# Who shifts the last rows: VectorE in place of ScalarE and GpSimd, and an earlier table load, in a two-layer kernel on one core

## The chip, the core and the metric

The kernel runs on one core of one Trainium2 chip. A core has a matrix engine (TensorE, PE in the profile), three engines for elementwise work (VectorE or DVE, ScalarE or ACT, GpSimd or POOL), SyncE (SP), which here only issues transfers, and 16 DMA engines that move data between the memory of the chip and the core. Each engine works through its own queue in order, and the engines wait for one another through semaphores. The metric is the device time of one execution in microseconds; lower is better.

## What is computed

Four sequences of 512 rows and 512 columns, all in 32-bit floats, go through two layers. The first is attention followed by two wide blocks with GELU; the second is an adapter whose weights are chosen per sequence by an index, with a residual and a normalisation over each row. Cut to what matters:

```python
def layer0(x, codes, Wq, Wk, Wv, Wp, bp, cW1, cb1, cW2, cb2, mW1, mb1, mW2, mb2):
    attn = softmax((x @ Wq) @ (x @ Wk).T * 512 ** -0.5)
    attn_out = attn @ (x @ Wv) @ Wp + bp
    cms_out = gelu(attn_out @ cW1 + cb1) @ cW2 + cb2 + one_hot(codes, 512)[:, None, :]
    modifier = gelu(concat([attn_out, cms_out]) @ mW1 + mb1) @ mW2 + mb2
    return clip(x + cms_out + modifier, 0.0, 1.0)

def layer1(stream, x, W_down, b_down, W_up, b_up, ln_w, ln_b):
    Wd, bd, Wu, bu, g, b = (p[stream] for p in (W_down, b_down, W_up, b_up, ln_w, ln_b))
    h = x + gelu(x @ Wd + bd) @ Wu + bu
    mean, var = h.mean(-1), h.var(-1)
    return (h - mean) * rsqrt(var + 1e-5) * g + b
```

The change lies in the last line of `layer1`: each row is shifted by its mean, scaled by `g` and by the reciprocal root of its variance, and `b` is added ("the shift").

## The kernel before, in words

The kernel works on the four sequences in two pairs. It computes the products of the first layer by nested seven-product schemes, so that sums and differences of blocks (on VectorE and GpSimd) take the place of part of the matrix work. For each pair the wide blocks follow one another, and behind them each of the pair's two sequences goes through the adapter. The adapters of the first pair are spread between the matrix work of the second pair. Those of the second pair stand at the end of the program: one is begun inside the last wide block (`adapter`, lines 1534 to 1545, sequence 3), and the other, sequence 2, comes after everything else (`last_adapter`, lines 1547 to 1557). That last one is the sequence of the change.

An adapter first applies the down projection and a GELU (`down`, line 1483: four matmuls per tile on TensorE, then the GELU on ScalarE at line 1493). In the last sequence the tokens are halved, so there are four GELUs of 128 x 256. Then come four row tiles of 128 rows each. For each tile, `up` (line 1495) has TensorE add the turned residual and the up projection in a bank of PSUM, and VectorE take the statistics (lines 1514 and 1516) and write (h - mean) * g to SBUF in one instruction (line 1517). Next `normalised` (line 1520) has ScalarE take the root of the variance (line 1523) and VectorE its reciprocal (line 1526). What follows depends on the tile:

- tiles 0, 1 and 2: ScalarE multiplies the 128 x 512 tile by the reciprocal root (line 1530), then GpSimd adds `b` (line 1531);
- tile 3 (`t == NT - 1`): VectorE does both in one instruction (line 1528).

Last, the tile of 256 KB is sent to the output (line 1532). In the second pair the issuing engine is SyncE, and its eight issues stand in its queue in the order of the tiles.

ScalarE needs a table of values for GELU and another for roots, and a load (ACT_TABLE_LOAD) stands in its queue where the function changes. In the last sequence the load for the roots is recorded with the first root at line 1523, behind the wait for that tile's statistics. A scheduler orders the queues of the engines; `tc.keep_in_program_order` keeps an instruction at the place where it was written. `touched` is a column of 128 values that is written once at the start and never read. The end of the program has line 1713: every engine drains its queue, SyncE waits for the outputs, and a barrier over all engines closes the program.

Of the kernel before, what the change touches and what calls it, by code (L numbers as in the profile page):

```python
# [10 lines left out]
AF = mybir.ActivationFunctionType  # L11
# [7 lines left out]
def kernel(  # L19
# [38 lines left out]
    nc = tc.nc  # L58
# [5 lines left out]
    NT = T // P  # L64
# [16 lines left out]
    def bank(name):  # L81
        return psum.tile([P, 512], F32, tag="bank", name=name)
# [100 lines left out]
    eps = const.tile([P, 1], F32, name="eps")  # L183
    nc.vector.memset(eps, EPS)

    touched = const.tile([P, 1], F32, name="touched")
# [1291 lines left out]
    def with_bias(y, bu, y1):  # L1478

        for c in range(NV):  # L1480
            nc.scalar.activation(y1[:, c, :], y[:, c, :], AF.Identity, bias=bu[:, c : c + 1])

    def down(y, wd, bd, g, n, tokens=slice(0, 512)):
        ps = bank("down_ps")[:, : tokens.stop - tokens.start]
        for c in range(NV):
            nc.tensor.matmul(  # L1486
                ps,
                lhsT=wd[:, c, n * P : (n + 1) * P],
                rhs=y[:, c, tokens],
                start=(c == 0),  # L1490
                stop=(c == NV - 1),
            )
        nc.scalar.activation(g[:, n, tokens], ps, AF.Gelu, bias=bd[:, n : n + 1])

    def up(g, wu, y1, aff, h, t):


        ps = bank("up_ps")
        for c in range(NV):
            nc.tensor.matmul(  # L1500
                ps[:, c * P : (c + 1) * P], lhsT=y1[:, c, t * P : (t + 1) * P], rhs=ident,
                is_transpose=True, start=(c == 0), stop=True, skip_group_check=True,
            )
        for n in range(NB):
            nc.tensor.matmul(  # L1505
                ps,
                lhsT=g[:, n, t * P : (t + 1) * P],
                rhs=wu[:, n, :],
                start=False,
                stop=(n == NB - 1),  # L1510
                skip_group_check=True,
            )
        stats = small.tile([P, 6], F32, name="stats")
        nc.vector.bn_stats(stats, ps)
        mv = small.tile([P, 2], F32, name="mv")
        nc.vector.bn_aggr(mv, stats)
        nc.vector.scalar_tensor_tensor(h, ps, mv[:, 0:1], aff[:, 0, :], ALU.subtract, ALU.mult)
        return mv

    def normalised(b, h, mv, aff, t, eng, last=False):  # L1520

        rstd = small.tile([P, 1], F32, name="rstd")
        root = nc.scalar.activation(rstd, mv[:, 1:2], AF.Sqrt, bias=eps)
        if last:
            tc.keep_in_program_order(root)
        nc.vector.reciprocal(rstd, rstd)
        if t == NT - 1:
            nc.vector.scalar_tensor_tensor(h, h, rstd, aff[:, 1, :], ALU.mult, ALU.add)
        else:
            nc.scalar.activation(h, h, AF.Copy, scale=rstd)  # L1530
            nc.gpsimd.tensor_tensor(h, h, aff[:, 1, :], ALU.add)
        eng.dma_start(out=out[b, t * P : (t + 1) * P, :], in_=h)

    def adapter(b, y, loaded, g, rows, y1, eng):

        wd, wu, bd, bu, aff = loaded
        for n in range(NB):
            down(y, wd, bd, g, n)
            yield
        with_bias(y, bu, y1)  # L1540
        yield
        for t in range(NT):
            mv = up(g, wu, y1, aff, rows[:, t, :], t)
            normalised(b, rows[:, t, :], mv, aff, t, eng)
            yield

    def last_adapter(b, y, loaded, g, rows, y1, eng):

        wd, wu, bd, bu, aff = loaded
        with_bias(y, bu, y1)  # L1550
        first_half, second_half = slice(0, 256), slice(256, 512)
        for tokens in (first_half, second_half):
            for n in range(NB):
                down(y, wd, bd, g, n, tokens)
        for t in range(NT):
            mv = up(g, wu, y1, aff, rows[:, t, :], t)
            normalised(b, rows[:, t, :], mv, aff, t, eng, last=True)
# [14 lines left out]
    for pair in range(B // 2):  # L1572
# [87 lines left out]
        if final:  # L1660
            for _ in one:
                pass
            adapt(0, spaces[0], nc.sync, kind=last_adapter)
        else:
            load(0, 6)
            c1_rhs = next_rhs[0]
            extra = adapters()
# [49 lines left out]
```

## Time and profile before

| what | us |
|---|---|
| three runs | 1176.99, 1177.01, 1180.69 |
| median of the runs | 1177.01 |
| the profiled execution, its own time | 1178.76 |
| span of the profiled execution (first to last instruction) | 1176.8 |
| busy in the span: TensorE matmuls | 1163.0 (99%) |
| busy: VectorE | 880.6 (75%) |
| busy: GpSimd | 578.2 (49%) |
| busy: ScalarE | 297.4 (25%) |

The granted TensorE clock was 0.998 of full speed. A line of the profile's timeline gives the start in the span, the busy time, the engine, the line of the program, the operation, the tile written and the tiles read, and the count; in brackets stands the idle time before it and what ended it. A line of the chain gives a start, a time, and what that time was spent on. A row for one source line gives the engine (with a q for the engine's instruction queue alone), the operation, the count, the shortest, median and longest duration in ns, and the first and last start in us.

### The profile page before, as it was taken

What the parts mean: (1) busy time and instruction counts of PE and PEld (TensorE: products, weight loads), DVE (VectorE), ACT (ScalarE), POOL (GpSimd) and SP (SyncE); (2) the same over time, 40 slices, a digit from 0 to 9 for tenths busy, and PEclk for the clock granted to TensorE, in tenths of its full rate; (3) what the DMA queues carried; (4) which work ended last, traced back from release to release, by engine and by line L of the source; (5) the groups of instructions that cost most, each with busy time, mean ns of one, the idle gap of its engine ahead of it and who ended that gap; (6) DMA issues with size and microseconds to landing.
All of it is one profiled execution on the core that took longest, in us unless ns stands there. A gap on an engine that the chain in (4) does not pass through costs nothing.

```text
span 1176.8 us, 13556 instructions
## 1 busy us (share of the span) xinstructions
PE 1163.0 (99%) x4937; PEld 918.0 (78%) x4937; DVE 880.6 (75%) x1192; ACT 297.4 (25%) x540; POOL 578.2 (49%) x634
## 2 busy tenths in 40 slices
PE   9999999999999999999999999999999999999996
PEld 8588558657468888888888877748888888888874
DVE  5745655587699867899699956769994588689954
ACT  4235315236520000013310036380000003220024
POOL 4989999988986057997400723630000001143002
PEclk9999999999999999999999999999999999999999
DMA  9642784897766588999937654262745364684701
GB/s 337 254 147 107 285 338 162 298 398 269 265 251 244 185 271 313 339 366 330 294 127 303 198 179 170 83 195 107 287 146 193 145 243 151 187 296 173 239 1 71
DMA packets 82609, 263.07 MB, mean 224 GB/s; under 512 B 8132, under 2 KB 37872, under 8 KB 67312
## 3 DMA queue, kind: packets, MB, share of 16 engines
q1 hardware_dynamic: 57184, 155.21, 36.8%
q0 software_dynamic: 23120, 97.57, 23.5%
q10 hardware_dynamic: 2240, 9.44, 2.0%
q8 instruction: 39, 0.64, 0.2%
q14 instruction: 26, 0.21, 0.1%
HBM read 190.88 MB, written 68.16 MB: 220 GB/s over the span
## 4 chain that ended last, share of the span: by engine, by line
PE 95%; DVE 2%; DMA 1%; ACT 1%; issue 0%
PE i L1380 29%; PE i L1282 26%; PE sum L704 9%; PE sum L638 8%; PE c L1214 8%; PE sum L1139 7%; PE up_ps L1505 2%; PE down_ps L1486 2%; PE tr_ps L490 1%; DMA wslot<-in_L_cond_mW 1%; PE up_ps L1500 1%; DVE hidden L548 1%; DVE slot L210 1%; PE tr_ps L869 0%; PE idle_ps L193 0%
## 5 line engine op out<-in xcount | busy, mean ns | idle before, releaser
L1282 PE MATMUL i<-slot,wslot 128*128 128x256 f32 x1184 | 261.8, 379 | 1.8 <-DVE part L1009 1.4
L1282 PEld LDWEIGHTS i<-slot,wslot 128*128 128x128 f32 x1184 | 224.6, 190 | 33.7 <-issue 2.4
L1380 PE MATMUL i<-slot,wslot 128*128 128x256 f32 x896 | 202.5, 379 | 0.0
L1380 PEld LDWEIGHTS i<-slot,wslot 128*128 128x128 f32 x896 | 170.2, 190 | 23.1
L1016 ACT COPY first<-i 128x256 f32<-128x256 f32 (+1 forms) x56 | 26.8, 478 | 523.7 <-PE i L1380 250.8
L1380 PE MATMUL i<-hidden,wslot 128*128 128x256 f32 x576 | 132.2, 379 | 0.0
L1380 PEld LDWEIGHTS i<-hidden,wslot 128*128 128x128 f32 x576 | 109.4, 190 | 16.2 <-issue 1.4
L1009 DVE TENSOR_TENSOR part<-i,part 128x512 f32<-128x512 f32 (+1 forms) x156 | 90.8, 592 | 39.1 <-PE i L1282 24.6
L1038 ACT ACTIVATE hidden<-hidden,bias 128x512 f32<-128x512 f32 x128 | 84.4, 716 | 76.4 <-DVE hidden L548 66.8
L1603 POOL DMA_DIRECT2D slot<-xT_kept x4 | 2.9, 715 | 165.2 <-PE i L1282 165.2
L1214 PE MATMUL c<-slot,wslot 128*128 128x512 f32 x160 | 69.2, 592 | 0.0
L210 DVE TENSOR_TENSOR slot<-hidden 128x1024 f32<-128x1024 f32 x48 | 62.2, 1296 | 0.0
L1606 POOL TENSOR_TENSOR cms<-cms,slot 128x512 f32<-128x512 f32 x16 | 26.0, 1643 | 70.9 <-PE i L1282 38.5
L1214 PEld LDWEIGHTS c<-slot,wslot 128*128 128x128 f32 x160 | 30.4, 190 | 38.3 <-issue 35.6
L210 DVE TENSOR_TENSOR slot<-hidden,slot 128x1024 f32<-128x1024 f32 x48 | 59.3, 1235 | 0.3
L1009 DVE TENSOR_TENSOR part<-i,first 128x512 f32<-128x512 f32 (+1 forms) x62 | 36.4, 591 | 28.6 <-PE i L1282 17.4
L548 DVE TENSOR_TENSOR sum<-sum,wslot 128x512 f32<-128x512 f32 x48 | 33.4, 697 | 31.0 <-PE sum L704 18.9
L548 DVE TENSOR_TENSOR hidden<-part,hidden 128x2048 f32<-128x2048 f32 x20 | 55.5, 2776 | 0.5
L704 PE MATMUL sum<-hidden,wslot 128*128 128x256 f32 x232 | 53.2, 379 | 0.0
L1139 PE MATMUL sum<-mod,wslot 128*128 128x256 f32 x224 | 51.8, 379 | 0.0
L704 PEld LDWEIGHTS sum<-hidden,wslot 128*128 128x128 f32 x232 | 43.8, 190 | 5.8
L1139 PEld LDWEIGHTS sum<-mod,wslot 128*128 128x128 f32 x224 | 42.6, 190 | 5.8
(329 smaller groups left out, 2099.8 us busy)
## 6 DMA issues: line engine op xcount, KB each, us to landing
wslot<-m_kept SPq DMA_DIRECT2D x48, 1024.0 KB
wslot<-m_kept SPq DMA_DIRECT2D x36, 512.0 KB
wslot<-c_kept SPq DMA_DIRECT2D x16, 1024.0 KB
slot<-in_L_cond_mW POOLq DMA_DIRECT2D x24, 512.0 KB
wslot<-in_L_cond_mW SPq DMA_DIRECT2D x24, 512.0 KB
wslot<-in_L_cond_cW SPq DMA_DIRECT2D x36, 256.0 KB
slot<-in_L_cond_cW POOLq DMA_DIRECT2D x16, 512.0 KB
m_kept<-wide POOLq DMA_DIRECT2D x6, 1024.0 KB
```

The source lines that it names most:

```text
L210: i = eng.tensor_tensor(out_, one, two, ALU.subtract)
L548: nc.vector.tensor_tensor(dst, a, b, ALU.add)
L638: nc.tensor.matmul(ps, lhsT=lhs[p][:, c, r * P : (r + 1) * P], rhs=rhs[p][:, c, :], start=(first_ and c == 0), stop=(c == 1), skip_group_c ...
L704: nc.tensor.matmul(v[:, j, :], lhsT=lhs[p][:, c, j * P : (j + 1) * P], rhs=rhs[p][:, c, :], start=(first_ and j == 0 and c == 0), stop=(c ...
L1009: nc.vector.tensor_tensor(dst, ps, other, ALU.add)
L1016: nc.scalar.copy(c1, p1)
L1038: nc.scalar.activation(block[:, t, :], block[:, t, :], AF.Gelu, bias=bias_c[:, 8 * half + t : 8 * half + t + 1],)
L1139: nc.tensor.matmul(halves_of(ps)[:, j, :], lhsT=a[g][:, at_[q], j * P : (j + 1) * P], rhs=rhs[q][:, 0, :], start=(first_ and j == 0), stop ...
L1214: nc.tensor.matmul(ps, lhsT=lhs(c, t), rhs=operands[p][:, c, :], start=(c == 0), stop=(c == 1),)
L1282: nc.tensor.matmul(out_ps[:, j, :], lhsT=a[j][q][:, c, :], rhs=now[q][:, c, :], start=(c == 0), stop=(c == 1),)
L1380: nc.tensor.matmul(ps[:, :256], lhsT=a[k // 2][q][:, k % 2, :], rhs=now[q][:, k, :], start=(k == 0), stop=(k == 3),)
L1606: nc.gpsimd.tensor_tensor(cms[s][:, d, :], cms[s][:, d, :], in_rows[3][:, d, :], ALU.add)
```

## The change

In the last sequence, VectorE's single instruction is used for tiles 1, 2 and 3 and no longer for tile 3 alone; tile 0 stays with ScalarE and GpSimd. And a root of the constant `eps` into `touched` is written behind the last GELU of the last sequence, kept at that place, so that the table for the roots is loaded there. The other three sequences are as before.

```diff
@@ normalised @@
         if last:
             tc.keep_in_program_order(root)
         nc.vector.reciprocal(rstd, rstd)
-        if t == NT - 1:
+        if t == NT - 1 or last and t > 0:
+
             nc.vector.scalar_tensor_tensor(h, h, rstd, aff[:, 1, :], ALU.mult, ALU.add)
         else:
             nc.scalar.activation(h, h, AF.Copy, scale=rstd)
@@ last_adapter @@
         for tokens in (first_half, second_half):
             for n in range(NB):
                 down(y, wd, bd, g, n, tokens)
+
+        tc.keep_in_program_order(nc.scalar.activation(touched, eps, AF.Sqrt))
         for t in range(NT):
             mv = up(g, wu, y1, aff, rows[:, t, :], t)
             normalised(b, rows[:, t, :], mv, aff, t, eng, last=True)
```

In the built program the order on TensorE and SyncE is unchanged. ScalarE has the table load and the added root directly behind the fourth GELU, and two multiplies fewer. VectorE has two more instructions, each behind its tile's reciprocal, and the reciprocal of tile 0 now stands ahead of the statistics of tile 1 and no longer behind them. GpSimd has two adds fewer.

## The prediction

> **What bounds the kernel now.** I read four views, from the whole to the end: the page, the chain of work that ended last, the instructions in order of time from 1158 us on, and the rows of line 1713, the closing of the program, in short windows. Where a view rounds a row to 0.1, I read its start from the trace to 0.01. The change touches nothing ahead of the last sequence's four row tiles, so only the last 18 us can move.
>
> The page puts the kernel on TensorE, and the chain says how that hands over at the end:
>
> ```profile
> span 1176.8 us, 13556 instructions
> ...
> PE 95%; DVE 2%; DMA 1%; ACT 1%; issue 0%
> ```
> ```profile
> 1165.67 1.73 PE up_ps L1505 x4
> 1167.41 0.02 issue
> 1167.43 0.71 DVE stats L1514
> 1168.14 0.02 issue
> 1168.17 0.19 DVE mv L1516
> 1168.36 0.03 issue
> 1168.38 0.36 DVE hidden L1517
> 1168.75 0.30 issue
> 1169.05 0.16 DVE rstd L1526
> 1169.21 0.03 issue
> 1169.24 0.75 DVE hidden L1528
> ```
>
> TensorE stops at 1167.41, and VectorE finishes tile 3 at 1169.24 + 0.75 = 1169.99. The span is 1176.8, so 6.8 us lie behind the last arithmetic, and the chain is silent on them. Line 1713 fills them:
>
> ```profile
> L1713 SPq EVENT_SEMAPHORE  x10: 17/28/28, 1170.4 to 1172.4; - x10
> L1713 SPq DRAIN  x2: 7/7/7, 1172.5 to 1172.5; - x2
> L1713 PEldq DRAIN  x1: 5360/5360/5360, 1162.1 to 1162.1; - x1
> L1713 POOLq DRAIN  x1: 8172/8172/8172, 1167.8 to 1167.8; - x1
> L1713 ACTq DRAIN  x1: 326/326/326, 1168.4 to 1168.4; - x1
> L1713 DVEq DRAIN  x1: 791/791/791, 1169.3 to 1169.3; - x1
> ```
>
> Here is the number that decides. Every engine drains before the closing barrier. SyncE, which waits for the last output to land, is through at 1172.5. ScalarE is through at 1168.7, VectorE at 1170.0, TensorE at 1167.5. GpSimd's drain takes 8.17 us and ends at 1167.85 + 8.17 = 1176.02; the barrier's first rows on GpSimd stand at 1176.1, the span's end at 1176.8. So **GpSimd's drain ends last, 3.5 us after SyncE**. The view of waits puts 3.7 us of SyncE's wait there down to TensorE's queue, which had been idle since 1167.5: the name is wrong, the wait is real.
>
> The drain is that of GpSimd's own queue. Its row starts when the last add (line 1531, tile 2) goes to the engine; that add runs from 1167.88 for 1.26 us, to 1169.14. The drain therefore lasts 6.87 us beyond the last add. The drain with which the program opens (line 1702) took 167 ns, so the long one is not a price of every drain; why this one is long, no row shows.
>
> **The change, part by part.** All durations are from the last tiles in order of time.
>
> *Table load.* Before, it stands behind the wait for tile 0's variance: 1161.96 to 1163.24. After, ScalarE issues it behind its last GELU (1158.81 + 0.47 = 1159.28): 1.28 us, then one 128x1 root of a constant, 0.29 (as the root at line 1523), done by about 1160.9. Tile 0's variance comes at 1161.88, so both are covered by 2.7 us of idle time that ScalarE has there; nothing but the roots is queued behind them. Tile 0's root runs at about 1161.97 to 1162.27 instead of 1163.25 to 1163.55.
>
> *Tile 0.* VectorE's shift-and-scale (line 1517) starts at 1161.92 as before; the reciprocal follows 0.67 later, as on tile 2 (1166.23 to 1166.90), ending at 1162.74. ScalarE's multiply then takes 0.72 (1162.77 to 1163.49) and GpSimd's add 1.26: **1163.57 to 1164.83**. It is now GpSimd's last work. Before, GpSimd ended at 1169.14; it ends 4.3 us earlier. In the program's order VectorE's reciprocal of tile 0 now stands ahead of tile 1's statistics, so it could hold them; it ends 0.4 before they can start (1163.12, set by TensorE).
>
> *Tiles 1 and 2.* Removed: two ScalarE multiplies (0.72 each) and two GpSimd adds (1.26 each). Added: two VectorE instructions of the form at line 1528, 0.75 each. Tile by tile VectorE now needs what tile 3 took, 1167.43 to 1169.99 = 2.56, against TensorE's 2.16 per tile (1163.12, 1165.28). So VectorE falls behind. Tile 1: 1163.12 to 1165.68. Tile 2's statistics do not depend on the row ahead of them; they start between 0.08 before it ends (as the reciprocal at 1169.05 does before 1169.13) and 0.04 after: 1165.60 to 1165.72, and the tile ends at 1168.16 to 1168.28. Tile 3 likewise starts at 1168.08 to 1168.32 and ends at **1170.64 to 1170.88**, 0.65 to 0.89 later than before. I take 0.7, since the pipelined start is what a pair with no dependence shows. The roots stay hidden beside the shift-and-scale (0.3 beside 0.67).
>
> *Outputs.* All eight output issues of the last pair are on SyncE, in order; tiles 1 and 2 now wait for VectorE instead of GpSimd. Issues: 1164.9, 1165.7, 1168.2, 1170.7. Each of these transfers moves data for about 0.85 us, starting 0.85 after its issue (windows from 1166.5 on), so the last one was not queued before and is not after. No other queue is touched: GpSimd issues no DMA here, and its indirect loads ended at 1092.
>
> *The end.* SyncE: from the last row of VectorE to its drain 1172.55 - 1169.99 = 2.56, so 1170.7 + 2.56 = 1173.26. GpSimd: 1164.83 + 6.87 = 1171.70, now 1.6 us early. SyncE ends last. From the later of the two to the span's end it was 1176.8 - 1176.02 = 0.78; the span becomes 1174.0, **2.8 us less**.
>
> So the change loses 0.7 us on the chain that the profile names and gains 3.5 on the one it does not. The profiled execution took 1178.76 for its span of 1176.8 (1.96 around it), 1.75 above the median of the three runs, 1177.01. 1178.76 - 2.8 = 1175.96 for an execution like that one; from the median, **1174.3** (2.76 less, rounded up).
>
> Unknown is the drain's rule. From the nearest rows its excess lies between 0.05 (the opening one, which ended at 0.49, behind a last memset that ended at 0.44) and 6.87; only an excess above 1173.26 - 1164.83 = 8.4 would make it bind again. I take 6.87, from the same place in the same program.
>
> The Trainium skill (VectorE: DVE Perf Modes, The DRAIN you can't avoid) speaks against this: it calls the drains at a program's start and end boilerplate of about 12 ns on all five engines. By that rule GpSimd's drain would cost nothing, SyncE would have closed the program before as well, and the sum would be +0.7 instead of -2.8. The trace has 7 ns for SyncE's and 8172 ns for GpSimd's, so for GpSimd the forecast follows the row; what is left of the rule is in the first rival.
>
> **Rivals.**
> - *The drain follows something common, not GpSimd's last add* (slower): it ended 3.5 after SyncE's and 6.0 after VectorE's last row, and one execution cannot tell these distances apart. If it keeps one of them, the whole end moves with VectorE's tile 3 by 0.7: 1177.7. It decides whenever the drain ends more than 1.6 us later than 1171.7. For it: nothing shows what the drain does for 6.87 us. Against: the profile shows no wait of it for another engine, and nothing else runs between 1172.6 and 1176.0 that could release it. Chance 0.13. (A drain that costs nothing by itself and only shows the wait for such a common thing, as the rule above would have it, is this case too.)
> - *The drain is tied to the last add, but not by a steady 6.87*: shorter in the timed runs than in the profiled one (which took 1.75 more than their median), so that less was there to gain, or longer now. Half the gain: 1175.8. Chance 0.12.
> - *The change does not do what it says*: the built order shows the load directly behind the fourth GELU and the three rows on VectorE. Were the load still late, GpSimd's add would end 1.1 later and its drain at 1172.8, still ahead of SyncE's 1173.3, so the time would be the same 1174.3. Chance 0.02, counted with the forecast.
> - *Something outside the change*: one of the three runs shown is 1180.69, 3.7 above the others; a median drawn there gives about 1178. Chance 0.05.
>
> **How the numbers follow.** The forecast, 1174.3, has 0.70, with its own range 1173.6 to 1175.0 (0.65 to 0.89 on VectorE, some tenths for the landing and the barrier). To leave no more than 2 in 10 out the range must reach the first rival: 1173.5 to 1177.8. 0.3% is 3.5 us, about what a measurement of this kernel can tell from no change, and the most that this change can gain is those 3.5 us if VectorE lost nothing. So faster by over 0.3% has 0.10 (the forecast, if the drain was longer in the runs than in the profile), slower 0.04 (most of the last rival), within it the remaining 0.86.
>
> **What would show it.** GpSimd's last add near 1163.6, its drain ending near 1171.7; VectorE's last row ending at 1170.6 to 1170.9; SyncE's drain near 1173.3, now the last; a span of 1174.0. If GpSimd's drain still ends after SyncE's, the step "6.87 behind the last add" is wrong. If VectorE ends later than 1170.9, something holds it that I don't see: GpSimd's tile 0 add, which ends 0.1 before tile 1's new row starts, is the candidate.

## The result, and the profile after

| | before | after |
|---|---|---|
| median of 22 runs each, us | 1177.0 | 1176.03 |
| lowest and highest run | 1176.15 to 1180.69 | 1173.07 to 1178.75 |
| profiled execution | 1178.76 | 1176.32 |
| its span | 1176.8 | 1174.2 |

The ratio of the runs is 0.998, with a 95% interval of 0.9972 to 0.9989: a gain of 0.1 to 0.3%, within the 0.3% that the prediction could not tell from no change. The two medians alone would give 0.9992, which lies outside that interval; the section on the other two microseconds says why. The forecast was 1174.3 in a range of 1173.5 to 1177.8. The median lies in the range, 1.7 above the forecast.

The page of the kernel after gives the span:

```profile
span 1174.2 us, 13555 instructions
```

The chain of waits of the kernel after, its last pieces (start, time, what it was spent on):

```profile
1167.66 0.75 DVE hidden L1529
1168.42 0.62 DVE stats L1514
...
1170.03 0.08 DVE rstd L1526
1170.11 0.02 issue
1170.13 0.75 DVE hidden L1529
```

Before, the chain went from TensorE's four matmuls into the statistics of tile 3. Now a row of VectorE (tile 2's, line 1529) stands ahead of those statistics: VectorE is the engine that is late in the last tiles, as the working said. VectorE ends at 1170.13 + 0.75 = 1170.88, where it had ended at 1169.99.

The closing of the program, now line 1716, in a window from 1160 to 1173.6 us:

```profile
L1716 SPq DRAIN  x2: 7/7/7, 1173.4 to 1173.4; - x2
L1716 POOLq EVENT_SEMAPHORE  x2: 17/17/17, 1173.4 to 1173.5; - x2
L1716 POOLq DRAIN  x1: 8182/8182/8182, 1163.8 to 1163.8; - x1
```

GpSimd's drain is as long as before (8182 ns, 8172 before) but starts 4.0 us earlier, at 1163.805. It ends at 1171.99, and SyncE's drain, at 1173.42, is now the last. The barrier's rows on GpSimd follow at once; before, SyncE was through at 1172.5 and the barrier had to wait until 1176.0 for GpSimd.

The timeline of the kernel after, the rows that the change moved:

```profile
1159.57 1.28 ACT L1557 ACT_TABLE_LOAD   x1
1160.87 0.20 ACT L1557 ACTIVATE touched<-eps 128x1 f32<-128x1 f32 x1
...
1163.84 1.27 POOL L1532 TENSOR_TENSOR hidden<-hidden,wide 128x512 f32<-128x512 f32 x1 [9.94 <-ACT hidden L1531]
...
1165.20 0.75 DVE L1529 SCALAR_TENSOR_TENSOR hidden<-hidden,rstd,wide 128x512 f32<-128x512 f32 x1
```

The load stands in idle time ahead of tile 0's statistics (1161.24 here). GpSimd's one add ends at 1165.12, and the first of VectorE's new rows starts 0.08 behind that end. This neighbourhood will matter.

**A ruler for the rest.** The statistics of tile 0 in the last sequence (line 1514) are the first instruction that any of these changes can delay. I call what lies ahead of that row *the head* and what lies from its start to the span's end *the tail*:

| profiled execution | head | tail | GpSimd's drain ends | SyncE's drain |
|---|---|---|---|---|
| before | 1160.97 | 15.84 | 1176.02 | 1172.55 |
| after | 1161.24 | 12.96 | 1171.99 | 1173.42 |

The tail became 2.88 shorter. The raw spans differ by 2.6 because the head came out 0.27 longer, and it holds the same instructions in both kernels, but for the early load and its root, which run while ScalarE has nothing else to do.

### The profile page after: what moved, and what is told of

Same layout as the page of the kernel before. It is cut to its first block, busy times and chain, and to the rows that moved or that the text cites. A ratio compares the mean times of both kernels' runs of the same rounds, so it can differ in the third digit from the quotient of the medians.

```text
span 1174.2 us, 13555 instructions
## 1 busy us (share of the span) xinstructions
PE 1163.1 (99%) x4937; PEld 918.1 (78%) x4937; DVE 876.7 (75%) x1194; ACT 296.3 (25%) x539; POOL 574.2 (49%) x632
## 4 chain that ended last, share of the span: by engine, by line
PE 94%; DVE 2%; DMA 2%; ACT 1%; issue 0%
PE i L1380 29%; PE i L1282 25%; PE sum L704 9%; PE sum L638 8%; PE c L1214 8%; PE sum L1139 7%; PE down_ps L1486 2%; DMA wslot<-in_L_cond_mW 2%; PE up_ps L1505 2%; PE tr_ps L490 1%; DVE hidden L548 1%; DVE slot L210 1%; PE up_ps L1500 1%; PE tr_ps L869 0%; PE idle_ps L193 0%
```

## The experiments

My theory: GpSimd's drain closes the program, 6.87 behind GpSimd's last add, so what helps is that GpSimd stops early; the table load is worth nothing by itself. The rivals: the early load carries part of the gain; and the drain follows something other than GpSimd's own last work. A second set of questions is what the 6.87 us are. Twelve kernels ran. All times of the large kernels' ends are given as tails.

### The two halves of the change

The early load alone, from the kernel after:

```diff
-        if t == NT - 1 or last and t > 0:
+        if t == NT - 1:
```

> The table load behind the last GELU is kept; the tiles 0, 1 and 2 are shifted by ScalarE and GpSimd as before. Theory (GpSimd's closing drain ends 6.9 us behind its last add, and that drain ended last before): GpSimd's last add is again that of tile 2, ending near 1169.1, since tile 2 waits for TensorE and not for the table; its drain ends near 1176.0; the time is that of the kernel before, within 0.3 us. Rival (the earlier table is what shortened the kernel): about 2.6 us below the kernel before, as the changed kernel.

The tail is 15.84, that of before to 0.01. The drain of GpSimd (its closing is line 1715) binds as before:

```profile
L1715 SPq DRAIN  x2: 7/7/7, 1173.8 to 1173.9; - x2
L1715 POOLq DRAIN  x1: 8175/8175/8175, 1169.2 to 1169.2; - x1
```

SyncE is through at 1173.9, GpSimd at 1177.39. The median of 12 runs is 1177.12 against 1178.59 for before on that chip (31 runs); the ratio, 0.9991, has an interval of 0.9978 to 1.0003, which includes 1 but reaches down to the rival's 2.6 us. So it is the tail, and not the runs, that settles it: the load alone gains nothing there.

The rows alone, with the table load where it was, behind the wait for tile 0's variance:

```diff
-        tc.keep_in_program_order(nc.scalar.activation(touched, eps, AF.Sqrt))
```

> VectorE shifts the tiles 1, 2 and 3; the table load is back behind the wait for tile 0. Theory: GpSimd's last add (tile 0) ends 1.1 us later than in the changed kernel, near 1166.0, its drain near 1172.9, still ahead of SyncE's 1173.4; the time is that of the changed kernel, within 0.3 us, 2.6 below the kernel before. Rival (the earlier table is what shortened the kernel): the time of the kernel before, or 0.7 above it.

The tail is 13.81, 2.03 better than before but 0.85 worse than after. My expectation missed this. (The runs, with a median of 1176.68 and a ratio of 0.9985, 0.9973 to 0.9996, do not tell it from the change.) The timelines of GpSimd and of VectorE in this kernel show why:

```profile
1164.89 1.26 POOL L1532 TENSOR_TENSOR hidden<-hidden,wide 128x512 f32<-128x512 f32 x1 [11.09 <-ACT hidden L1531]
```
```profile
1165.23 1.47 DVE L1529 SCALAR_TENSOR_TENSOR hidden<-hidden,rstd,wide 128x512 f32<-128x512 f32 x1
1166.63 0.69 DVE L1514 BATCH_NORM_STATS2 stats<-up_ps 128x6 f32<-128x512 f32 x1
```

With the late load, GpSimd's add of tile 0 comes some 1.1 later relative to VectorE and lies beside tile 1's row. The row takes 1.47 instead of 0.75. It also starts 0.13 later than in the kernel after, since with the late load ScalarE's root of tile 1 comes later; so the statistics of tile 2 behind it start 0.86 late, 0.72 of it from the stretch. VectorE, which has no slack in these tiles, carries that to the end: SyncE's drain stands at 1174.19, the drain of GpSimd at 1173.03. In the kernel after, the same row starts 0.08 behind the end of the add and takes 0.75. So the load does have a worth, but mainly not the one that its place suggests: it takes GpSimd's add out of VectorE's way.

The Trainium skill (SBUF — State Buffer, SBUF: two separate sides) states a rule for such pairs: VectorE and GpSimd share one pair of ports to SBUF, as a lock that is held for a whole instruction, and it applies to a VectorE operation with two SBUF inputs against a GpSimd operation that reads SBUF. These two rows are such a pair, and the trace agrees for the most part: of the 0.92 us that the row lay beside the add, it lost 0.72, where a full block would have cost all of it.

### Does the drain follow GpSimd's last work?

The kernel after, and behind the last tile a copy of one column on GpSimd, which has to wait for VectorE's last row:

```diff
             normalised(b, rows[:, t, :], mv, aff, t, eng, last=True)
+        late = const.tile([P, 1], F32, name="late")
+        tc.keep_in_program_order(nc.gpsimd.tensor_copy(late, rows[:, NT - 1, 0:1]))
```

> The changed kernel, with one more GpSimd instruction: a copy of one column (128x1) of tile 3 behind VectorE's last row, into a column that nobody reads. Theory (the drain costs 6.9 behind whatever GpSimd did last): the copy ends near 1171.1, the drain near 1178.0, the span is 1178.8: 4.6 us above the changed kernel and 2.0 above the kernel before. Rival (the long drain belongs to the 128x512 adds, or its length counts from something else than the last instruction): the copy costs some tenths, the drain ends by 1172, the time is that of the changed kernel.

The timeline and the closing rows (line 1718) of this kernel:

```profile
1171.70 0.18 POOL L1562 COPY late<-hidden 128x1 f32<-128x1 f32 x1 [5.84 <-DVE hidden L1529]
```
```profile
L1718 SPq DRAIN  x2: 7/7/7, 1174.1 to 1174.2; - x2
L1718 POOLq DRAIN  x1: 7080/7080/7080, 1171.7 to 1171.7; - x1
```

The copy takes 0.18 us and ends at 1171.88; the drain ends at 1178.75, 6.87 behind it. The tail is 17.56, 4.60 more than after. The median of 11 runs is 1180.68, a ratio of 1.0027 to before (1.0015 to 1.0039): the interval lies above 1, so **a copy of 128 numbers costs some 0.3%**. The excess of 6.87 is thus, in this program, fixed in length and tied to the end of whatever GpSimd does last; it does not keep a distance from VectorE or SyncE, which was the first rival.

### What are the 6.87 us?

Three ideas: A, the drain cleans up behind the transfers that GpSimd issued; B, it is a price of GpSimd's computing as such; C, of code that GpSimd had to load. Five small kernels only double x, and leave all the rest of the computation out. Each loads the four sequences, adds every tile to itself on GpSimd, and lets SyncE write the outputs:

```diff
 # m1: loads by SyncE
+        nc.sync.dma_start(out=rows, in_=x[b].rearrange("(t p) v -> p t v", p=128))
+        for t in range(4):
+            nc.gpsimd.tensor_tensor(rows[:, t, :], rows[:, t, :], rows[:, t, :], ALU.add)
 # m2: the four loads by GpSimd
-        nc.sync.dma_start(out=rows, ...
+        nc.gpsimd.dma_start(out=rows, ...
 # m3: m1 with an identity made on GpSimd at the start
+    make_identity(nc, ident)
 # m4: m2 with each load issued four times
+        for _ in range(4):
 # m5: m1 with the first sequence loaded by 64 transfers of 16x256 on GpSimd
+            nc.gpsimd.dma_start(out=rows[...], in_=x[...])
```

> A kernel that leaves the whole computation out and only doubles x: SyncE loads x, GpSimd adds each 128x512 tile to itself (16 adds), SyncE writes the output. No DMA is issued by GpSimd. Theory A (the 6.87 us behind GpSimd's last instruction are what it takes to settle GpSimd's own DMA queue): the drain ends within 0.2 us of the last add. Theory B (the price comes with compute on GpSimd as such): 6.87 behind the last add.

> As the kernel that doubles x (the rest of the computation is left out), but the four loads are issued by GpSimd and not by SyncE. Theory A (settling GpSimd's own DMA queue): the drain ends 6.87 behind the last add. Theory C (it comes with the code loaded for a select on GpSimd, as the identity matrix of the full kernel needs): within 0.2.

> As the kernel that doubles x with loads by SyncE (the rest of the computation is left out), but GpSimd also builds the identity matrix at the start, with the pool configuration that the full kernel has there. Theory A (own DMA queue): within 0.2 of the last add. Theory C (loaded code): 6.87.

> As the kernel that doubles x with its loads on GpSimd (the rest of the computation is left out), but each of the four loads is issued four times: 16 loads, 4 times the packets of GpSimd's DMA queue (1088 there, so 4352). The drain ended 0.07 us behind the last add without loads on GpSimd, 0.41 with the four, and 6.87 in the full kernel with its 23120 packets in 206 transfers. Theory P (the drain pays per packet that GpSimd's queue moved in the whole program, 0.29 to 0.32 ns each): 1.35 to 1.5 behind the last add. Rival (a step that comes with the first use of the queue, 0.35): 0.41 again.

> As the kernel that doubles x (the rest of the computation is left out), with three of the loads on SyncE and the first one cut into 64 transfers of 16x256 on GpSimd. Theory P (per packet, about 2000 here): 0.6 to 0.75 behind the last add. Theory N (per transfer, 0.086 us each as with four loads): 5.6.

The closing drain of m1, and GpSimd's last adds from its timeline:

```profile
L70 POOLq DRAIN  x1: 4122/4122/4122, 26.9 to 26.9; - x1
```
```profile
26.93 4.02 POOL L23 TENSOR_TENSOR rows<-rows 128x512 f32<-128x512 f32 x4 [8.80 <-DMA rows<-in_x]
```

As in the large kernel, the drain's row begins when the last adds go to the engine, so what counts is its end less the end of the last add: 31.025 - 30.958 = 0.067. The same reading of m4 and m5, whose drains are these:

```profile
L71 POOLq DRAIN  x1: 6120/6120/6120, 64.3 to 64.3; - x1
```
```profile
L79 POOLq DRAIN  x1: 17214/17214/17214, 40.6 to 40.6; - x1
```

| kernel | transfers by GpSimd | their packets | excess behind the last add, us | one run, us |
|---|---|---|---|---|
| m1 | 0 | 0 | 0.067 | 37.88 |
| m3 | 0 | 0 | 0.067 | 37.53 |
| m2 | 4 | 1088 | 0.413 | 38.84 |
| m4 | 16 | 4352 | 1.392 | 75.95 |
| m5 | 64 | 2048 | 5.302 | 60.37 |

B and C fall with m1 and m3. Of A it holds that the excess grows with the transfers that GpSimd issued; what the drain does for each, no row shows. Its size was missed: m2 was to have all 6.87 by A, or at most 0.2 by C, and had 0.413. m4 fitted a price per packet, and m5, which has fewer than half of m4's packets and four times its transfers, took that back (5.302, where packets gave 0.6 to 0.75 and transfers 5.6). So what is counted is the transfer: (1.392 - 0.413) / 12 = 0.0816 and (5.302 - 1.392) / 48 = 0.0815 us for each **transfer**, for those of 1 MB in m4 and those of 16 KB in m5 alike.

The kernel before has 206 transfers issued by GpSimd. To test the count in it, one line puts the eight outputs of the first pair on SyncE:

```diff
-                yield from adapt(s, (first, part, cms[s]), nc.gpsimd)
+                yield from adapt(s, (first, part, cms[s]), nc.sync)
```

> The kernel before, but the eight outputs of the first pair of sequences are issued by SyncE and not by GpSimd; at 144 packets each GpSimd's queue has 1152 fewer of 23120. Nothing is changed in the last sequence. Theory P (per packet, 0.293 ns): GpSimd's drain ends 6.53 behind its last add and not 6.87. Theory N (per transfer, 206 of them, 0.033 us each): 6.61. Rival (a constant of this program's end): 6.87.

```profile
L1713 POOLq DRAIN  x1: 7520/7520/7520, 1215.9 to 1215.9; - x1
```

The drain ends at 1223.41 and the last add at 1217.19, so the excess fell from 6.873 to 6.219. That is 0.654 / 8 = 0.0817 per transfer, the same slope as in the small kernels, and more than either reading had expected. (GpSimd's queue has 640 packets fewer, 80 for each output and not the 144 of the expectation; a price per packet would have to be 1.0 ns here and was 0.3 in m4.) But the level does not fit: 206 x 0.0815 would be 16.8, and 6.87 pays for some 83. In both kernels some 123 transfers would cost nothing (206 - 83, and 198 - 75). If these are the first ones, the paid ones begin near 420 us in both; which ones they are, and why, was not tried, and stays open.

The kernel itself became much slower, 1225.98 in one run against 1177.45. The view of SyncE's waits shows a new line:

```profile
SPq L1532 <- POOL part L1531: 58.2, 6, 31.9
```

SyncE's queue also issues the weights. Six of the moved outputs wait in it for GpSimd's adds, 58.2 us in total, and the weights queue behind them. TensorE falls 50 us behind between 720 and 810 us, and 2 at most anywhere else. A queue in order is a poor place for a transfer with a late input, even if it is cheaper at the end.

### Simpler and further versions

If GpSimd is to stop early, tile 0 can go to VectorE as well. With the early load, and then without it:

```diff
 # e3
-        if t == NT - 1 or last and t > 0:
+        if t == NT - 1 or last:
 # e5: that, and also
-        tc.keep_in_program_order(nc.scalar.activation(touched, eps, AF.Sqrt))
```

> VectorE shifts tile 0 too, so GpSimd has no work at all in the last sequence; its last add is that of the sequence before, ending near 1153.6. Theory: its drain ends near 1160.5, 6.9 behind that add, and is far from the end; VectorE carries 0.75 more and ends 0.3 later than in the changed kernel (the stats of tile 1 start 0.3 late), so the time is 0.3 above the changed kernel. Rival (the drain keeps a place near the end whatever GpSimd did last): a drain that ends near 1172, the time the same.

> VectorE shifts all four tiles of the last sequence (no GpSimd add there), and the table load is back behind the wait for tile 0. The stretch from the first statistics of the last sequence to the span's end was 15.84 us before, 12.95 in the changed kernel, 13.81 with the late load and tile 0 on GpSimd (there VectorE's row of tile 1 took 1.47 us instead of 0.75, beside GpSimd's add). Theory (that row was held by GpSimd's add; the late table alone costs little): no row over 0.8 us, VectorE ends 0.3 later than in the changed kernel, stretch 13.2 to 13.3. Rival (the late table itself costs the 0.86, by making the chain of VectorE late): 13.8 or more.

The tails are 13.01 and 12.94, against 12.96 after. Two things had been mis-sized. A fourth row on VectorE cost 0.05 and not 0.3: tile 1's and tile 2's statistics do start 0.32 late in e3, but the scheduler put tile 3's statistics ahead of tile 2's row, and rows that do not depend on one another overlap there by 0.08 where dependent ones stood 0.03 to 0.04 apart, which won 0.27 back. And the late load cost nothing in e5, where the scheduler changed VectorE's order once more. VectorE's timeline in e5 has no stretched row:

```profile
1162.18 0.73 DVE L1528 SCALAR_TENSOR_TENSOR hidden<-hidden,rstd,wide 128x512 f32<-128x512 f32 x1
...
1163.56 0.68 DVE L1514 BATCH_NORM_STATS2 stats<-up_ps 128x6 f32<-128x512 f32 x1
1164.15 0.74 DVE L1528 SCALAR_TENSOR_TENSOR hidden<-hidden,rstd,wide 128x512 f32<-128x512 f32 x1
```

Without an add on GpSimd the late load is free, and with one (the rows alone, above) it costs 0.85. So the load matters mainly through the add's place; the order of VectorE's rows differs too, and no run keeps it fixed. GpSimd's drain now ends at 1158.4 in e3 and 1158.7 in e5, over 12 us ahead of SyncE's: the rival of e3, a drain that stays near the end, falls. Medians: 1174.14 (9 runs, 0.9973, 0.9961 to 0.9985) and 1173.99 (12 runs, 0.9974, 0.9960 to 0.9988). Their intervals overlap that of the change, and the tails agree to 0.05, so neither tells them apart; e5 is the simplest of the three, with one edited line.

Last, e5 with tile 3's row in two halves, each sent by an issue of its own:

```diff
+        if last and t == NT - 1:
+            for at in (0, V // 2):
+                half = slice(at, at + V // 2)
+                nc.vector.scalar_tensor_tensor(
+                    h[:, half], h[:, half], rstd, aff[:, 1, half], ALU.mult, ALU.add
+                )
+                eng.dma_start(out=out[b, t * P : (t + 1) * P, half], in_=h[:, half])
+            return
```

> The kernel in which VectorE shifts all four tiles and the table load stays behind the wait for tile 0, with the last tile finished in two halves of 256 columns, each sent to the output by itself. Theory (SyncE's last landing is now what ends the program): the last transfer is 128 KB and not 256, 0.43 us shorter, and VectorE ends at about the same time (0.42 + 0.42 less 0.08 of overlap, instead of 0.75); the stretch from the first statistics of the last sequence to the span's end goes from 12.94 to 12.5 to 12.65, 3.2 to 3.3 below the kernel before. Rival (the landing is a fixed latency, or something else ends the span): 12.94 or, with one more wait at SyncE, 13.0.

```profile
1173.99 0.88 DVE L1530 SCALAR_TENSOR_TENSOR hidden<-hidden,rstd,wide 128x256 f32<-128x256 f32 x2
```

The tail is 12.82, 0.12 less than e5: between the rival (12.94) and the expectation (12.5 to 12.65). The halves took 0.88 together and not 0.76, and from the last issue SyncE waited 1.81 for the landing instead of 2.02. By the runs (1175.72, ratio 0.9972, 0.9959 to 0.9985) it cannot be told from e5.

### Where the other two microseconds went

The tail became 2.9 shorter, and the median 0.97. The list of the runs explains the difference, for they lie in two bunches:

| | lower bunch | its median | upper bunch | its median |
|---|---|---|---|---|
| before | 13 runs, 1176.15 to 1177.01 | 1176.63 | 8 runs, from 1178.62 | 1178.90 |
| after | 9 runs, 1173.07 to 1174.44 | 1173.83 | 13 runs, from 1175.71 | 1176.50 |

(One run of before, 1177.64, lies between.) Bunch against bunch the gain is 2.80 and 2.40, near what the tail gives. But the median of before falls in its lower bunch and that of after in its upper one, and so it moved by 0.97 only; the mean of the runs moved by 1.99. In e3 and e5 the jump goes the other way: their medians lie 4.5 and 5.2 below those of before on the same chip, with tails only 2.8 and 2.9 shorter. Why fewer runs of after lie in the lower bunch, chance or not, no run shows.

What sets the profiled executions apart lies mostly in the head. Its instructions are the same in all these kernels, but for that load and root, and it took 1158.84 (e3) to 1165.11 us (e7) in the profiles: a spread of 6 us ahead of the change. Two places make most of it. The first is near 484 us. VectorE and GpSimd in the kernel after, then VectorE in e3:

```profile
483.82 6.72 DVE L548 TENSOR_TENSOR hidden<-part,hidden 128x2048 f32<-128x2048 f32 x1
490.58 2.70 DVE L548 TENSOR_TENSOR hidden<-hidden,hidden 128x2048 f32<-128x2048 f32 x1
```
```profile
485.37 2.34 POOL L362 TENSOR_TENSOR wide<-slot 128x1024 f32<-128x1024 f32 x1
```
```profile
483.27 3.78 DVE L548 TENSOR_TENSOR hidden<-part,hidden 128x2048 f32<-128x2048 f32 x1
487.08 4.32 DVE L548 TENSOR_TENSOR hidden<-hidden,hidden 128x2048 f32<-128x2048 f32 x1
```

The first of two adds of VectorE took 6.72 in the one and 3.78 in the other (2.78 in the mean of the 20 of its form in the kernel after), beside adds of GpSimd: the pattern of the stretched row again, in large. In e3 the second was stretched in turn, 4.32 in place of 2.70, so the pair was through 1.3 sooner and not 2.9. Six profiles (before, after, e1, e2, e4 and e7) have the long first add, 6.55 to 6.91. In these TensorE waits 1.3 to 1.6 us near 501.5, and there they fall 1.5 to 1.9 behind e3. e3 and e5 (3.78 and 3.65) have no such wait, and these are the two whose profiled runs, 1173.65 and 1173.90, lie in their lower bunch. What differs there is GpSimd's add near 485: in the six it starts just before the one ahead has ended, in e3 and e5 0.60 and 0.07 behind that end, and it takes 3.8 and 4.3 us in these two where it takes 2.3 in the six. It seems that then VectorE's add goes first. The second place is in the chain of waits of e7:

```profile
509.15 15.16 DMA wslot<-in_L_cond_mW
```

There TensorE waits for weights, and falls 4.2 us behind. Smaller differences arise ahead of 100 us (up to 0.8) and between 550 and 700 (up to 1.3, in e1). None of these places lies near the change, and no run here altered one of them alone; that they make the spread, and the first the two bunches (which lie 2.3 and 2.7 apart, more than its 1.5 to 1.9), is read from these traces and not shown.

## Why the prediction was right or wrong

*GpSimd's drain closes the program, and frees the end when GpSimd stops early*: right, and shown in both directions (e4 makes it late again by a 128x1 copy, e1 leaves it late). Its excess behind GpSimd's last operation was 6.873 before, 6.872 after, and 6.87 in e1, e2, e3, e4, e5 and e7, so the second rival, an unsteady drain, fell with the first. SyncE became last, with GpSimd's drain 1.4 us ahead of it (predicted 1.6).

*The Trainium skill's rule* (VectorE: DVE Perf Modes, The DRAIN you can't avoid: about 12 ns for the boilerplate drains on all five engines). SyncE's 7 ns are near it, and VectorE's drain, whose row of 791 ns begins with its last work as GpSimd's does, ended 0.05 us behind that work. GpSimd's drain comes near it only with no transfers of its own (0.067 behind the last add, m1). Everywhere else the row decides; the forecast by the rule, 0.7 slower, fell.

*VectorE loses 0.65 to 0.89, taken as 0.7*: it ended 9.65 behind tile 0's statistics, 9.02 before, so 0.62 was lost. That is 0.03 under the low end of the range, which stands for statistics that start 0.08 ahead of the end of the row; those of tile 2 do just that.

*SyncE's drain 2.56 behind VectorE's last row*: 1173.42 - 1170.88 = 2.54. *Barrier 0.78*: 1174.19 - 1173.42 = 0.77. *The span 2.8 less*: the tail 2.88 less, the raw span 2.61.

*The load costs nothing and gains nothing* (the rival "the change does not do what it says" gave the same 1174.3 for a late load): wrong by 0.85. The working asked only whether GpSimd's drain would still be ahead of SyncE's. It would (e2: 1173.03 against 1174.19), but the later add lies beside VectorE's row, and the root of tile 1 comes 0.1 later. The prediction's last sentence named this pair as the candidate, though it had no price for it.

*The total*: the step that failed is the last term, "from the median, 1174.3", with its premise that "only the last 18 us can move". It set the 2.76 against the median of three runs as if the head were fixed. The tail gave 2.88, but the median of 22 runs moved by 0.97, because the head varies by more than the gain. The 1177.01 of the three runs belongs to the lower bunch of before; 1174.3 is thus a forecast for the lower bunch of after, which came out at 1173.83, while the median of all runs fell in the upper one. The median, 1176.03, is outside the forecast's own range (1173.6 to 1175.0). It lies in the wide one because that had been stretched to the first rival, which did not happen, and that is luck. So is its nearness to the second rival's 1175.8 (half of 2.76 would in fact give 1175.6). The forecast from the profiled execution (1175.96) was nearer to its own counterpart, 1176.32, which has the 0.27 of a longer head in it.

## What to carry to other kernels

Read the closing of the program as a stage of its own: list when each engine's drain ends, and compare GpSimd's with that of the engine that sends the last output; the chain of waits said nothing of it here. If GpSimd issues transfers, let its last operation, however small, end several microseconds ahead of the last output (here 6.87 ahead of SyncE's drain, which is 4.3 ahead of the end of VectorE's last row), and move its last work to an engine that is needed until then anyway. When a gain is a few microseconds out of a thousand, measure it from an instruction just ahead of the change to the end, since the part ahead may vary by more than the gain from one execution to the next. And look at the list of the runs: where they lie in two bunches, the median can jump from one to the other.

## What the runs showed of the hardware that was not expected

- In the small kernels the closing drain of GpSimd costs 0.0815 us for each transfer that GpSimd issued (0.067, 0.413, 1.392 and 5.302 us for 0, 4, 16 and 64), for 1 MB and 16 KB alike. In the large kernel the slope is the same (0.0817, from one run), but the excess pays for some 83 of 206 transfers; which rule picks them is open.
- A 128x512 row of VectorE that reads two SBUF tiles took 1.47 us instead of 0.75 beside an add of GpSimd, and 0.75 when it started 0.08 behind that add.
- A half of that row (128x256) takes 0.48, more than half of 0.75; splitting the last output gained 0.12 us of tail.
